# A conditioned transformer block on one core: gate rows over four column groups, and rules of their own for 13 of 64 attention steps

## The chip, the cores and the metric

The kernel runs on one core of a Trainium2 chip. The metric is the device time of one execution in microseconds (us). TensorE is written PE (PEld is its weight load), VectorE is DVE, ScalarE is ACT, GpSimd is POOL and SyncE is SP; SP issues the DMAs.

## What is computed

A transformer block whose two layer norms and two residual additions are modulated by a condition vector, one for each batch row. x is 8 x 1024 x 512, the condition 8 x 512, all in fp32; there are 16 heads of 32.

```python
mod = silu(condition) @ Wada + bada                # 8 x 3072
sh_a, sc_a, gt_a, sh_m, sc_m, gt_m = split(mod, 6, axis=1)
xm = layernorm(x) * (1 + sc_a[:, None]) + sh_a[:, None]
x  = x + gt_a[:, None] * attention(xm)             # causal, 16 heads; its output is @ Wproj + bproj
xm = layernorm(x) * (1 + sc_m[:, None]) + sh_m[:, None]
x  = x + gt_m[:, None] * (gelu(xm @ W1 + b1) @ W2 + b2)
```

The change touches how gt_a and gt_m, the two rows called gates, are made, and in which order the instructions of some attention steps are issued. What is computed stays the same.

## The kernel before, in words

**Tiling.** The tokens are worked through in 16 blocks of 512: block n is half n % 2 of batch row n // 2. Each block has four attention steps (n, g), g = 0 to 3, of four heads each, 64 steps in all. Beside attention there is linear work: the products for q, k and v, for the projection and for the two layers of the MLP. They are made as Strassen products from sums of weight quarters and sums of activations, by the helper `matmul` (L233), which puts four products on the four column groups of PE's array, 32 output rows each.

**An attention step.** It makes scores to find the row maxima: `scores_at_once` (L1784) multiplies on PE (L1791), adds the causal mask on DVE (L1805) and reduces on DVE (L1808). `split_maxima` (L1813) splits the maxima into three bf16 parts with four small operations (L1827 to L1830) on POOL or DVE, whichever the model says is done sooner. `maxima_rows` (L1838) turns them to rows on PE (L1846). `weights_T` (L1861) makes the scores again, transposed, with the maxima subtracted by a product of their own (L1872, L1884), and ACT takes the exponential (L1897); POOL clears the part over the diagonal (L1902). `weigh` (L1914) multiplies by v (L1925). POOL adds up the weights (`add_weights`, L2010), and `finish` (L1935) makes the denominators on PE (L1946). A "unit" is one such tile of scores or weights.

**PSUM.** Scores and transposed scores share one tile of four banks, called st, so they take turns; the output of `weigh` has one bank (po); linear work, maxima rows, denominators and gates share three banks.

**What sets the order.** The order of instructions on every engine is fixed when the program is built. While it issues instructions, the kernel's Python keeps a model of the time at which each engine is free (`now`, `note` and its kin, `due`, L70 to L160). Three rules in it matter here.

- `either` (L179) puts an elementwise sum on DVE or POOL. It goes to DVE only if DVE would be done earlier by more than `margin`, 1000 ns (L186); in the last step the margin is -2000.
- `step_aside` (L1651) is called ahead of each group of attention's instructions on PE. While the modelled wait of that group (`own`) is longer than that of the linear work that is ready (`other`), it issues linear work first. When linear work is behind its due time, attention goes ahead only if `other > own + 100`, and otherwise if `own <= max(other, 50)`.
- The list `plan` (L281) says in which window of blocks each linear step and each gate is made, and `costs` (L370) what each is reckoned at.

**The gates.** `gates` (L565) runs twice, for kinds a and m, during the first steps of block 0. It multiplies the activated condition (8 rows, as weights of 128 x 8) by the raw weights, in eight products of 256 columns, all on one column group and with 8 rows of output (L582). The bias comes by DMA as an 8-row broadcast (L571), is added on DVE while the bank is read (L222), and for kind a a second row, gate times the projection's bias (L574), is made on DVE. The rows are kept in DRAM, and `gate_broadcasts` (L598) loads the row of one batch row to all 128 partitions, 256 KB at a time: two rows for a and one for m, for each of 8 batch rows. `settle` (L1337) multiplies the MLP's output by the gate and adds it to the residual, both through `either`.

Of the kernel before, what the change touches and what calls it, by code (L numbers as in the profile page):

```python
# [22 lines left out]
def kernel(  # L23
# [128 lines left out]
    def note_pe(ns, form, reads=(), writes=()):  # L152
        now["PE"] = max(now["PE"], due(reads, writes))
        if shape[0] != form:
            shape[0] = form
            now["PE"] += SWITCH
        note("PE", ns, reads)
        spent[0] += ns
        for k in writes:
            written[k] = now["PE"] + PIPE  # L160
# [15 lines left out]

    margin = [1000]

    def either(out, a, b, op, reads, writes):  # L179

        n = 1
        for d in out.shape[1:]:
            n *= d
        on_dve, on_pool = 60 + 1.24 * n, 120 + 2.28 * n
        t = due(reads, writes)
        if max(now["DVE"], t) + on_dve + margin[0] < max(now["POOL"], t) + on_pool:  # L186
            nc.vector.tensor_tensor(out, a, b, op)
            note("DVE", on_dve, reads, writes, port=True)
        else:
            nc.gpsimd.tensor_tensor(out, a, b, op)  # L190
            note("POOL", on_pool, reads, writes)
# [29 lines left out]
    def combine_out(out, bank, src, other, reads=(), writes=(), op=ALU.add, last=True):  # L221
        nc.vector.tensor_tensor(out, src, other, op)  # L222
        note("DVE", 690, [("l", bank), *reads], writes)
        live[bank] = not last
# [142 lines left out]
        return []  # L367

    order = [at for w in range(-1, NB + 1) for step in plan[w] for at in pieces_of(step)]
    costs = {"at": 16 * TR, "mt": 16 * TR, "gates": 4 * MM, "mod": 4 * MM}  # L370
    costs["at"] = 0
    costs.update({kind: 14 * MM for kind in ("k", "q", "v", "u", "proj")})

# [181 lines left out]
    def half(i, size):  # L555
        return slice(i * size, (i + 1) * size)
# [8 lines left out]
    def gates(kind):  # L565

        i, bias = GATES[kind]
        at = take(4)
        part = {kf: halves(j) for kf, j in zip(RAW, at)}
        b_gate = tmp.tile([P, D], F32, tag="y", name=f"b_gate_{kind}")[:B, :]  # L570
        nc.sync.dma_start(b_gate, bada[i * D : (i + 1) * D].unsqueeze(0).to_broadcast([B, D]))  # L571
        if bias is not None:
            b_out = tmp.tile([P, D], F32, tag="y", name=f"b_out_{kind}")[:B, :]
            nc.sync.dma_start(b_out, bias.unsqueeze(0).to_broadcast([B, D]))  # L574
        yield [], [BANK]
        bank = lin_bank()
        ps = banks[bank][:B, :]
        for fh in range(2):
            for k in range(NC):
                if fh + k:  # L580
                    yield [], []
                nc.tensor.matmul(  # L582
                    ps[:, half(fh, HB)], condT[:, k, :B], part[k // 2, fh][:, k % 2, :],
                    start=fh + k == 0, stop=k == NC - 1, skip_group_check=True,
                )
                note_pe(2 * COLUMN * HB, "columns", [], [("l", bank)])
        release(*at)
        combine_out(b_gate, bank, ps, b_gate)
        made = [(f"g{kind}", b_gate)]
        if bias is not None:  # L590
            nc.vector.tensor_tensor(b_out, b_out, b_gate, ALU.mult)
            note("DVE", 700, port=True)
            made.append((f"gb{kind}", b_out))
        for name, row in made:
            kept_rows[name] = kept.tile([B, D], F32, tag=f"kept_{name}", name=f"kept_{name}")
            nc.sync.dma_start(kept_rows[name], row)

    def gate_broadcasts(b, kind):  # L598

        for name in [name for name in (f"g{kind}", f"gb{kind}") if name in kept_rows]:  # L600
            row = rowp.tile([P, D], F32, tag=f"row{name}", name=f"row_{name}_{b}")
            nc.sync.dma_start(row, kept_rows[name][b : b + 1, :].to_broadcast([P, D]))
            gate_rows[name] = row


# [577 lines left out]
        return y_keys[kind]  # L1183
    LANDING = 6000

    def add_to(xt, other, reads, writes, op=ALU.add):
        either(xt, xt, other, op, [*reads, *writes], writes)

    def half_sums(n, t):

# [146 lines left out]
    def settle(n, f, t, y, ky):  # L1337

        c = half(f, HB)
        gate = gate_rows["gm"][:, c].unsqueeze(1).to_broadcast([P, 2, HB])  # L1340
        keys = [("xr", n, 2 * t), ("xr", n, 2 * t + 1)]
        add_to(y, gate, [("row", "gm")], [ky], ALU.mult)
        add_to(residual[n][:, half(t, 2), c], y, [ky], keys)

    def store(n, t):
        b, h = blocks[n]
# [300 lines left out]
    def until(condition):  # L1647
        while not condition():
            work()

    def step_aside(reads, writes):  # L1651


        while threads():
            if linear_wait() == NEVER:
                hurry()
            own, other = wait_of((reads, writes)), linear_wait()
            if done_linear[0] < stream["due"]:
                if other > own + 100:
                    break  # L1660
            elif own <= max(other, 50):
                break
            work()
        while BANK in writes and bank_at() == NEVER:
            work()
        run_jobs()
        run_pool_jobs()
        run_transfers()
        run_preparation()
# [2 lines left out]


    TRIANGLE = [[0], [1, 3], [2]]
    groups = [(n, g) for n in range(NB) for g in range(NC)]

    def score_units(n, g):
# [335 lines left out]
    def attend():  # L2013
        previous = None
        for n in range(NB):
# [21 lines left out]
            written["free for k", n + 1] = 0.0  # L2037
            written["free for xr", n - 1] = 0.0
            for g, k, n_slots, upto in slots:
                if (n, g) == groups[-1]:  # L2040
                    margin[0] = -2000
                parts = weight_units(n, g)[k]
                while rows_due and any((n, part[3]) not in m_rows for part in parts):
                    maxima_rows()
                pT, slot = weights_T(n, g, parts)
                run_excursions(1)
                pace(exp_need(parts))
                maxima_rows()
                if previous is not None:
                    close(*previous)  # L2050
                for i in (n, n + 1) if h == 0 else (n,):
                    written["free for v", i] = 0.0
                if k > 0:
                    add_weights(n, g, [part for part in parts if part[3] == g], pT, slot)
                previous = (n, g, parts, pT, slot, k == n_slots - 1)
                if (n, g, k) == (0, NC - 1, n_slots - 1):

                    next_scores()
                    close(*previous)
                    previous = None  # L2060
                while unit_at[0] < upto:
                    ns = score_need(*units[unit_at[0]])
                    next_scores()
                    if h == 0:
                        run_excursions(1)
                    pace(ns)
                if previous is None:
                    maxima_rows()
# [125 lines left out]
```

## Time and profile before

| | us |
| --- | --- |
| median of 3 runs | 3460.41 |
| lowest and highest | 3459.74, 3460.67 |
| the profiled execution's own time | 3463.39 |
| span of its profile | 3461.7 |
| granted TensorE clock | 1.00 |

The span goes from the first to the last instruction that the profiler recorded; the execution's own time lies 1.7 us around it. A row of a timeline gives start, length, engine, line of the kernel, operation, output<-inputs, shapes and count; in square brackets stands how long the engine sat idle before it and what released it. Matmuls overlap, so their starts are the better measure of how fast they follow each other. An fp32 product counts as two instructions on PE. "Idle time" of a group is that of its engine just before it.

### The profile page before, as it was taken

Reading aid. Unit: us, or ns where it says so; the run is one execution under the profiler, and the core shown is the slowest. Engines: PE = TensorE matmul, PEld = TensorE weight load, DVE = VectorE, ACT = ScalarE, POOL = GpSimd, SP = SyncE. Lnnn points to the kernel's source line nnn. Section 1 sums busy time; section 2 is a strip of 40 time slices with the busy share of each in tenths; the row PEclk is TensorE's granted clock in tenths of the full one; section 3 lists DMA queues with packets and bytes.
Section 4 is the critical chain, followed back from the end, with each engine's and each line's share of the span. In section 5 each row is a group of like instructions: output and inputs, shape, how many; then the busy total and the mean of one; then the engine's idle time right before and its main releaser. Section 6 shows DMA issues by size and latency. Waiting matters only on the chain.

```text
span 3461.7 us, 122760 instructions
## 1 busy us (share of the span) xinstructions
PE 3420.8 (99%) x55538; PEld 1775.8 (51%) x55538; DVE 2068.1 (60%) x2304; ACT 1289.5 (37%) x1424; POOL 1939.0 (56%) x2092
## 2 busy tenths in 40 slices
PE   8999999999999999999999999999999999999999
PEld 5544554455544554455554455454554545545555
DVE  6765666646566465664657546575466755556454
ACT  2345244343243433434333352433524334242431
POOL 3666757756267472774626755277553775446520
PEclk9999999999999999999999999999999999999999
DMA  7832434345544455444544445444464444633344
GB/s 230 277 124 87 122 113 130 103 126 150 172 136 129 128 151 159 135 139 130 162 145 136 136 133 169 138 134 136 132 177 134 130 146 122 192 110 102 117 144 136
DMA packets 380429, 490.71 MB, mean 142 GB/s; under 512 B 28436, under 2 KB 236364, under 8 KB 379908
## 3 DMA queue, kind: packets, MB, share of 16 engines
q1 hardware_dynamic: 379712, 482.59, 46.4%
q8 instruction: 437, 7.16, 0.8%
q14 instruction: 84, 0.69, 0.1%
q10 hardware_dynamic: 196, 0.28, 0.0%
HBM read 429.22 MB, written 53.53 MB: 139 GB/s over the span
## 4 chain that ended last, share of the span: by engine, by line
PE 89%; DVE 4%; DMA 3%; ACT 2%; issue 1%; POOL 1%; SPq 0%; DVEq 0%; ACTq 0%; POOLq 0%
PE bank L233 61%; PE sc L1791 8%; PE po L1925 7%; PE st L1884 7%; PE st L1872 3%; DVE mx L1808 2%; PE bank L1946 2%; DMA w<-kept_up_S 1%; ACT pT L1897 1%; DMA xm_m<-turned_m 1%; DVE sc L1805 1%; PE bank L1846 1%; DVE hT L1378 0%; ACT hT L1309 0%; PE bank L887 0%
## 5 line engine op out<-in xcount | busy, mean ns | idle before, releaser
L2010 POOL TENSOR_TENSOR pT<-pT,pT 128x256 f32<-128x256 f32 (+3 forms) x1254 | 1218.8, 1007 | 159.6 <-ACT pT L1897 121.9
L1897 ACT ACTIVATE pT<-st 128x2048 f32<-128x2048 f32 x288 | 541.1, 1879 | 1007.8 <-PE st L1884 892.6
L233 PE MATMUL bank<-w,hT 128*32 128x256 f32 x14336 | 814.4, 380 | 0.0
L1808 DVE TENSOR_REDUCE mx<-sc 128x4 f32<-128x2048 f32 (+3 forms) x384 | 665.5, 1754 | 196.3 <-PE sc L1791 190.2
L233 PEld LDWEIGHTS bank<-w,hT 128*32 128x32 f32 x14336 | 453.8, 110 | 357.8 <-issue 74.2
L233 PE MATMUL bank<-xm_m,w 128*32 128x256 f32 x8192 | 499.2, 380 | 1.5 <-issue 1.0
L233 PE MATMUL bank<-t_m,w 128*32 128x256 f32 x6144 | 383.8, 380 | 0.8 <-DMA w<-kept_up_S 0.4
L1902 POOL TENSOR_SCALAR_AFFINE_SELECT pT<-pT 128x512 f32<-128x512 f32 x256 | 181.0, 725 | 359.0 <-ACT pT L1897 357.3
L233 PEld LDWEIGHTS bank<-xm_m,w 128*32 128x32 f32 x8192 | 255.5, 110 | 229.9 <-issue 64.3
L1791 PE MATMUL sc<-kT,qT 32*128 32x512 f32 (+3 forms) x3072 | 329.1, 520 | 3.2 <-DVE mx L1808 3.0
L1805 DVE TENSOR_TENSOR sc<-sc,mask 128x1024 f32<-128x1024 f32 (+1 forms) x160 | 162.7, 1017 | 250.5 <-PE sc L1791 174.0
L1925 PE MATMUL po<-pT,v 128*32 128x512 f32 (+3 forms) x3072 | 304.8, 491 | 0.0
L1884 PE MATMUL st<-qT,kT 32*128 32x512 f32 (+3 forms) x3072 | 300.0, 486 | 0.0
L233 PEld LDWEIGHTS bank<-t_m,w 128*32 128x32 f32 x6144 | 189.9, 110 | 177.3 <-issue 53.1
L233 PE MATMUL bank<-xm_a,w 128*32 128x256 f32 x3968 | 239.5, 380 | 1.8 <-ACT xm_a L902 1.1
L190 POOL TENSOR_TENSOR qT<-top,rec 128x512 f32<-128x512 f32 x59 | 77.3, 1310 | 280.5 <-ACT rec L1964 277.5
L222 DVE TENSOR_TENSOR hT<-bank,u_u 128x512 f32<-128x512 f32 x192 | 130.1, 686 | 150.4 <-PE bank L233 147.4
L1791 PEld LDWEIGHTS sc<-kT,qT 32*128 32x128 f32 x3072 | 129.4, 183 | 159.7 <-issue 58.0
L233 PE MATMUL bank<-w,qT 128*32 128x256 f32 (+1 forms) x3008 | 188.9, 389 | 2.3 <-DVE p_proj L214 2.3
L233 PE MATMUL bank<-t_a,w 128*32 128x256 f32 x2944 | 179.4, 380 | 0.0
L233 PEld LDWEIGHTS bank<-xm_a,w 128*32 128x32 f32 x3968 | 126.7, 110 | 98.0 <-issue 16.1
L1309 ACT ACTIVATE hT<-hT,cols 128x512 f32<-128x512 f32 x256 | 164.1, 711 | 23.1 <-DVE hT L222 22.4
(246 smaller groups left out, 3414.8 us busy)
## 6 DMA issues: line engine op xcount, KB each, us to landing
w<-in_L_cond_W_dram SPq DMA_DIRECT2D x384, 256.0 KB
w<-kept_up_S SPq DMA_DIRECT2D x256, 256.0 KB
w<-kept_down_S SPq DMA_DIRECT2D x256, 256.0 KB
w<-kept_qkv_S SPq DMA_DIRECT2D x180, 256.0 KB
w<-in_L_cond_Wqkv_dram SPq DMA_DIRECT2D x147, 256.0 KB
hat<-in_x_dram SPq DMA_DIRECT2D x64, 256.0 KB
xr<-in_x_dram SPq DMA_DIRECT2D x64, 256.0 KB
out_dram<-xr SPq DMA_DIRECT2D x64, 256.0 KB
```

The lines of the kernel that those rows point to most:

```text
L222: nc.vector.tensor_tensor(out, src, other, op)
L233: nc.tensor.matmul(ps[r], columns, rhs, start=start, stop=stop, skip_group_check=True)
L1309: nc.scalar.activation(hT[:, i, :], hT[:, i, :], AF.Gelu, bias=cols[:, O_B1 + f : O_B1 + f + 1])
L1791: nc.tensor.matmul(sc[:, j, c0 : c0 + w], qTs[n][r, gg, ts(qt, P)], keys_of(n, kh)[r, gg, :w], start=True, stop=True, skip_group_check=True,)
L1805: nc.vector.tensor_tensor(place, place, shape_of.to_broadcast(place.shape), ALU.add)
L1808: nc.vector.tensor_reduce(maxima[n, gg][:, kh, qt, :], sc[:, :, c0 : c0 + w], axis=AX.X, op=ALU.max)
L1872: nc.tensor.matmul(st[:, j, c0 : c0 + w], minus_ones[r, :], row[r, TB - w :], start=(c0 == 0), stop=False, skip_group_check=True,)
L1884: nc.tensor.matmul(st[:, j, c0 : c0 + w], kT[r, gg, ts(k % NTT, P)], qT[r, gg, TB - w :], start=False, stop=True, skip_group_check=True,)
L1897: nc.scalar.activation(pT[:, :, :used], st[:, :, :used], AF.Exp, scale=scale)
L1902: nc.gpsimd.affine_select(diagonal, diagonal, pattern=[[0, HPG], [1, P]], compare_op=ALU.is_ge, fill=0.0, base=0, channel_multiplier=-1,)
L1925: nc.tensor.matmul(po[r, TB - w :], v[:, k % NTT, g * P + j * hd : g * P + (j + 1) * hd], pT[:, j, c0 : c0 + w], start=(k == 0), stop=last ...
L2010: nc.gpsimd.tensor_tensor(into, into, pT[:, j, c0 : c0 + w], ALU.add)
```

## The change

It has four parts.

1. **Gates over four column groups.** `gates` makes, for each quarter of the columns, a product of 128 columns with 32 rows of output on its own column group (16 products for each kind, the condition now spread over all its 32 columns). The bias is no longer added on DVE: it comes by DMA as one row of 1 x 512 and is added by products with a row of ones (`spread_rows`, four products for each row; for kind a also four that spread the projection's bias beside it). DVE copies the 128 x 128 result, and for kind a multiplies the second by the first. The tile kept in DRAM is 128 x 128, and the broadcast of one batch row reads four pieces of 128 numbers. The planner reckons a gate at 2 MM in place of 4.
2. **Own rules for 13 steps.** `MANNER` gives 13 of the 64 steps a margin and a `leaning`. A leaning of 300 lets attention go ahead of linear work when its modelled wait is up to 300 ns longer than before the change. All other steps keep (1000, 0).
3. **Slack.** `either` can be given a `slack` that stands in for the margin.
4. `settle` uses a slack of 0 in block 0.

Below this text lines of after.py are some 17 to 22 higher than those of before.py from the attention on.

```diff
--- before.py
+++ after.py
@@ -176,14 +176,14 @@
 
     margin = [1000]
 
-    def either(out, a, b, op, reads, writes):
+    def either(out, a, b, op, reads, writes, slack=None):
 
         n = 1
         for d in out.shape[1:]:
             n *= d
         on_dve, on_pool = 60 + 1.24 * n, 120 + 2.28 * n
         t = due(reads, writes)
-        if max(now["DVE"], t) + on_dve + margin[0] < max(now["POOL"], t) + on_pool:
+        if max(now["DVE"], t) + on_dve + (margin[0] if slack is None else slack) < max(now["POOL"], t) + on_pool:
             nc.vector.tensor_tensor(out, a, b, op)
             note("DVE", on_dve, reads, writes, port=True)
         else:
@@ -367,7 +367,7 @@
         return []
 
     order = [at for w in range(-1, NB + 1) for step in plan[w] for at in pieces_of(step)]
-    costs = {"at": 16 * TR, "mt": 16 * TR, "gates": 4 * MM, "mod": 4 * MM}
+    costs = {"at": 16 * TR, "mt": 16 * TR, "gates": 2 * MM, "mod": 4 * MM}
     costs["at"] = 0
     costs.update({kind: 14 * MM for kind in ("k", "q", "v", "u", "proj")})
 
@@ -567,39 +567,56 @@
         i, bias = GATES[kind]
         at = take(4)
         part = {kf: halves(j) for kf, j in zip(RAW, at)}
-        b_gate = tmp.tile([P, D], F32, tag="y", name=f"b_gate_{kind}")[:B, :]
-        nc.sync.dma_start(b_gate, bada[i * D : (i + 1) * D].unsqueeze(0).to_broadcast([B, D]))
-        if bias is not None:
-            b_out = tmp.tile([P, D], F32, tag="y", name=f"b_out_{kind}")[:B, :]
-            nc.sync.dma_start(b_out, bias.unsqueeze(0).to_broadcast([B, D]))
+        added = [("g", bada[i * D : (i + 1) * D])] + ([] if bias is None else [("gb", bias)])
+        rows = []
+        for name, v in added:
+            row = tmp.tile([P, TB], F32, tag="y", name=f"b_{name}{kind}")[:1, :]
+            nc.sync.dma_start(row, v.unsqueeze(0))
+            rows.append(row)
         yield [], [BANK]
         bank = lin_bank()
-        ps = banks[bank][:B, :]
-        for fh in range(2):
-            for k in range(NC):
-                if fh + k:
-                    yield [], []
+
+        def spread_rows(r, start, stop):
+            for j in range(HPG):
                 nc.tensor.matmul(
-                    ps[:, half(fh, HB)], condT[:, k, :B], part[k // 2, fh][:, k % 2, :],
-                    start=fh + k == 0, stop=k == NC - 1, skip_group_check=True,
+                    banks[bank][j * hd : (j + 1) * hd, ts(r, P)], ones[:1, :hd], rows[r][:, ts(j, P)],
+                    start=start, stop=stop, skip_group_check=True,
                 )
-                note_pe(2 * COLUMN * HB, "columns", [], [("l", bank)])
+            note_pe(2 * COLUMN * P, "columns", [], [("l", bank)])
+
+        for k in range(NC):
+            for j in range(HPG):
+                nc.tensor.matmul(
+                    banks[bank][j * hd : (j + 1) * hd, :P], condT[:, k, :],
+                    part[k // 2, j // 2][:, k % 2, ts(j % 2, P)],
+                    start=k == 0, stop=False, skip_group_check=True,
+                )
+            note_pe(2 * COLUMN * P, "columns", [], [("l", bank)])
+            yield [], []
         release(*at)
-        combine_out(b_gate, bank, ps, b_gate)
-        made = [(f"g{kind}", b_gate)]
+        for r in range(len(rows)):
+            spread_rows(r, r > 0, True)
+        made = tmp.tile([P, TB], F32, tag="y", name=f"gates_{kind}")
+        gate = made[:, :P]
+        nc.vector.tensor_copy(gate, banks[bank][:, :P])
+        note("DVE", 250, [("l", bank)], [("gates", kind)])
         if bias is not None:
-            nc.vector.tensor_tensor(b_out, b_out, b_gate, ALU.mult)
-            note("DVE", 700, port=True)
-            made.append((f"gb{kind}", b_out))
-        for name, row in made:
-            kept_rows[name] = kept.tile([B, D], F32, tag=f"kept_{name}", name=f"kept_{name}")
-            nc.sync.dma_start(kept_rows[name], row)
+            nc.vector.tensor_tensor(made[:, P : 2 * P], banks[bank][:, P : 2 * P], gate, ALU.mult)
+            note("DVE", 250, [("l", bank)], [("gates", kind)])
+        live[bank] = False
+        for r, (name, _) in enumerate(added):
+            there = kept.tile([P, P], F32, tag=f"kept_{name}{kind}", name=f"kept_{name}{kind}")
+            kept_rows[name + kind] = there
+            nc.sync.dma_start(there, made[:, ts(r, P)])
 
     def gate_broadcasts(b, kind):
 
         for name in [name for name in (f"g{kind}", f"gb{kind}") if name in kept_rows]:
             row = rowp.tile([P, D], F32, tag=f"row{name}", name=f"row_{name}_{b}")
-            nc.sync.dma_start(row, kept_rows[name][b : b + 1, :].to_broadcast([P, D]))
+            of_b = kept_rows[name].rearrange("(j r) c -> r j c", r=hd)[b]
+            nc.sync.dma_start(
+                row.rearrange("p (j c) -> p j c", c=P), of_b.unsqueeze(0).to_broadcast([P, NC, P])
+            )
             gate_rows[name] = row
 
 
@@ -1183,8 +1200,8 @@
         return y_keys[kind]
     LANDING = 6000
 
-    def add_to(xt, other, reads, writes, op=ALU.add):
-        either(xt, xt, other, op, [*reads, *writes], writes)
+    def add_to(xt, other, reads, writes, op=ALU.add, slack=None):
+        either(xt, xt, other, op, [*reads, *writes], writes, slack)
 
     def half_sums(n, t):
 
@@ -1339,8 +1356,9 @@
         c = half(f, HB)
         gate = gate_rows["gm"][:, c].unsqueeze(1).to_broadcast([P, 2, HB])
         keys = [("xr", n, 2 * t), ("xr", n, 2 * t + 1)]
-        add_to(y, gate, [("row", "gm")], [ky], ALU.mult)
-        add_to(residual[n][:, half(t, 2), c], y, [ky], keys)
+        slack = 0 if n == 0 else None
+        add_to(y, gate, [("row", "gm")], [ky], ALU.mult, slack)
+        add_to(residual[n][:, half(t, 2), c], y, [ky], keys, slack=slack)
 
     def store(n, t):
         b, h = blocks[n]
@@ -1648,6 +1666,8 @@
         while not condition():
             work()
 
+    leaning = [0]
+
     def step_aside(reads, writes):
 
 
@@ -1656,9 +1676,9 @@
                 hurry()
             own, other = wait_of((reads, writes)), linear_wait()
             if done_linear[0] < stream["due"]:
-                if other > own + 100:
+                if other > own + 100 - leaning[0]:
                     break
-            elif own <= max(other, 50):
+            elif own <= max(other, 50) + leaning[0]:
                 break
             work()
         while BANK in writes and bank_at() == NEVER:
@@ -1672,6 +1692,7 @@
 
 
     TRIANGLE = [[0], [1, 3], [2]]
+    MANNER = {(0, 1): (1000, 300), (0, 3): (1000, 300), (1, 3): (-1000, 0), (2, 0): (-1000, 0), (2, 1): (2500, 0), (3, 1): (0, 0), (4, 0): (1000, 300), (6, 0): (1000, 300), (8, 0): (1000, 300), (10, 0): (1000, 300), (12, 1): (2500, 0), (14, 3): (0, 0), (3, 3): (2500, 300)}
     groups = [(n, g) for n in range(NB) for g in range(NC)]
 
     def score_units(n, g):
@@ -2037,6 +2058,7 @@
             written["free for k", n + 1] = 0.0
             written["free for xr", n - 1] = 0.0
             for g, k, n_slots, upto in slots:
+                margin[0], leaning[0] = MANNER.get((n, g), (1000, 0))
                 if (n, g) == groups[-1]:
                     margin[0] = -2000
                 parts = weight_units(n, g)[k]
```

## The prediction

> **What bounds the kernel now.** I read the head of the page first, then the chain that ended last.
>
> ```profile
> span 3461.7 us, 122760 instructions
> ...
> PE 3420.8 (99%) x55538; PEld 1775.8 (51%) x55538; DVE 2068.1 (60%) x2304; ACT 1289.5 (37%) x1424; POOL 1939.0 (56%) x2092
> ...
> PEclk9999999999999999999999999999999999999999
> ...
> PE 89%; DVE 4%; DMA 3%; ACT 2%; issue 1%; POOL 1%; SPq 0%; DVEq 0%; ACTq 0%; POOLq 0%
> ```
>
> TensorE (PE) is busy for 3420.8 of 3461.7 us, at full granted clock throughout, and the chain is PE for 89%. No other engine is above 60%. Only two things can shorten this program: less work on PE, or less of the 40.9 us in which PE stands idle. The busy times in three stretches (each row: length, then busy time and instructions of PE, PEld, DVE, ACT and POOL, clock, DMA share, GB/s) say where those 40.9 us lie.
>
> ```profile
> 0.00:89.20 89.20, 74.94 (x1196) 45.56 (x1197) 55.86 (x88) 24.89 (x35) 34.81 (x53) 1.00 0.69 227
> 89.20:3457.70 3368.50, 3345.82 (x54343) 1730.19 (x54342) 2011.42 (x2216) 1264.58 (x1389) 1904.20 (x2040) 1.00 0.47 139
> 3457.70:3461.70 4.00, 0.00 (x0) 0.00 (x0) 0.84 (x2) 0.00 (x0) 0.00 (x0) 1.00 0.52 195
> ```
>
> Start-up holds 14.3, the last store 4.0, and the 3368.5 us between them 22.7: over 64 attention steps about a third of a microsecond each. So the prize of any reordering is 22.7 us at most. The same view over the 13 steps that get rules of their own (the first of them, and the sum) says how much lies inside them.
>
> ```profile
> 89.20:115.80 26.60, 24.75 (x389) 13.54 (x389) 20.19 (x23) 9.69 (x12) 13.17 (x20) 1.00 0.78 261
> ...
> sum 537.20, PE 532.65 PEld 278.97 DVE 334.93 ACT 216.81 POOL 297.01; mean PE 40.97 PEld 21.46 DVE 25.76 ACT 16.68 POOL 22.85
> ```
>
> They lose 537.20 - 532.65 = 4.55 us in all. A rule also shifts what the next steps find, so what it is worth must be looked for behind its step as well. PE's waits, grouped (total us, times, longest), name the kinds:
>
> ```profile
> PE st L1872 <- DVE mx L1808: 8.1, 13, 1.9
> PE bank L1846 <- POOL mcols L1830: 5.9, 7, 1.6
> PE bank L233 <- DVE p_proj L214: 2.3, 5, 0.5
> ```
>
> The first is the shared score tile: PE may not write the next one before VectorE (DVE) has reduced the last. The second is the maxima rows, which wait for the split on GpSimd (POOL); the third is the projection, which waits for a copy out of PSUM.
>
> **The gate products, a term on PE alone.** The listing of line 582 and the timeline of PE (start, length to the modelled end, count) give both prices.
>
> ```profile
> L582 PE MATMUL bank<-w,condT x32: 378/379/383, 87.4 to 157.9; 128*8 128x256 f32 x32
> ```
> ```profile
> 90.84 1.67 PE L582 MATMUL bank<-w,condT 128*8 128x256 f32 x7
> 92.35 0.38 PE L582 MATMUL bank<-w,condT 128*8 128x256 f32 x1
> ...
> 104.79 0.72 PE L523 MATMUL bank<-w,condT 128*32 128x128 f32 x10
> 105.44 0.40 PE L1872 MATMUL st<-mrow,minus_ones 32*128 32x384 bf16 x8
> ...
> 1685.66 1.69 PE L233 MATMUL bank<-w,hT 128*32 128x256 f32 x28
> 1687.17 1.04 PE L1946 MATMUL bank<-pT,ones 128*32 128x512 f32 x8
> ...
> 2970.31 0.41 PE L1846 MATMUL bank<-ident_b,mcols 128*32 128x128 bf16 x16 [0.52 <-POOL mcols L1830]
> ```
>
> Removed: 32 instructions (each fp32 product is two) on one column group, a new one every 1.51/7 = 0.216 us: 6.9 us. Added: 16 + 16 products of 128 columns and 8 + 4 that spread the bias rows, 44 products or 88 instructions over four column groups. Such a mixture at 256 columns starts one every 1.51/28 = 0.054 us, so at 128 columns 0.027 (the maxima rows do 128 columns in 0.41/16 = 0.026): 2.4 us. The dearest row for 128 columns is line 523's, 0.65/10 = 0.065, a change of form included: 5.7 us. So the term lies between -1.2 and -4.5; I take **-4.5**, since the maxima rows are the nearest in width and in column groups.
>
> The Trainium skill (page "TensorE: Matmul & The Clock Gate", section "Back-to-back issue gap") gives about 81 ns for each 128-column matmul in a stream of weight load and matmul pairs. By it the 88 would take 7.1 us, an estimate from that page, and the gates would save nothing. The rows above disagree, with 0.026 and 0.027 where four column groups take turns.
>
> The two DVE operations per gate become 128x128 and cheaper. The broadcast reads four pieces of 512 B per partition in place of one of 2 KB: 24 loads of 128 x 3 more packets, 9216 on 380429. With the queue at 46.4% (row below) I cost that at nothing; its cover is the idle half of the queue. What is new is that PE reads the bias rows, which come by DMA:
>
> ```profile
> q1 hardware_dynamic: 379712, 482.59, 46.4%
> ```
> ```profile
> 80.25 2.05 SPq L990 DMA_DIRECT2D prep_up<-in_L_cond_W_dram  x4
> 82.39 0.41 SPq L393 DMA_DIRECT2D w<-kept_qkv_S  x1
> 82.84 0.33 SPq L571 DMA_DIRECT2D b_gate_a<-in_L_cond_bada_dram  x1
> 83.22 0.29 SPq L574 DMA_DIRECT2D b_out_a<-in_L_cond_bproj_dram  x1
> ```
>
> Five loads of 256 KB stand ahead of them: 1.3 MB at the 227 GB/s of that stretch is 5.8 us, so they land near 89; by the built order PE first needs them between 88 and 89, after the sixteen products. Behind a waiting product would stand all of PE. I bound this at 0 to 3 us for each gate and take 0: in the next stretch, quoted above, the queue moved 261 GB/s, by which they land near 88.2.
>
> **The moved steps.** In both programs I counted in the built order the PE work between the instruction that a waiter depends on and the waiter, with the spacings of the trace (0.054 us for a linear instruction, 1.14 for a score unit, 0.11 for a change of form, an estimate from 104.79: 0.65 less ten times 0.054). Where more lies between, the wait shrinks by as much. PE's order is the same in over twenty of the steps, and their waits are taken to stay. The waits with more work ahead of them:
>
> ```profile
> 115.81 0.40 PE L1872 MATMUL st<-mrow,minus_ones 32*128 32x512 bf16 x4 [1.87 <-DVE mx L1808]
> ...
> 444.59 0.64 PE L233 MATMUL bank<-xm_a,w 128*32 128x256 f32 x8 [0.70 <-ACT p_k L217]
> ...
> 794.76 0.64 PE L233 MATMUL bank<-w,qT 128*32 128x256 f32 x8 [0.48 <-DVE p_proj L214]
> ...
> 1327.31 1.14 PE L1791 MATMUL sc<-kT,qT 32*128 32x512 f32 x8 [2.02 <-DVE mx L1808]
> ...
> 1672.81 0.40 PE L1872 MATMUL st<-mrow,minus_ones 32*128 32x384 bf16 x8 [0.55 <-DVE mx L1808]
> ...
> 2495.61 0.64 PE L233 MATMUL bank<-w,qT 128*32 128x256 f32 x8 [0.48 <-DVE p_proj L214]
> 2522.05 0.40 PE L1872 MATMUL st<-mrow,minus_ones 32*128 32x384 bf16 x8 [0.56 <-DVE mx L1808]
> ...
> 2891.09 0.40 PE L1872 MATMUL st<-mrow,minus_ones 32*128 32x384 bf16 x8 [0.66 <-DVE mx L1808]
> ```
>
> - 115.81, step (0,2): 16 linear instructions and a change of form more, 0.97 of the 1.87 go.
> - 444.59, step (2,1): 32 linear instructions more, all 0.70 go.
> - 794.76 to 2495.61, four projections at the start of blocks 4, 8, 10 and 12: a score unit now comes between, 4 x 0.48 = 1.9 go.
> - 1327.31, step (6,2): 16 linear instructions more, 0.86 of 2.02 go.
> - 1672.81 to 2522.05, second step of blocks 8, 10 and 12: 56 to 72 more, 3 x 0.56 = 1.7 go.
> - 2891.09, step (14,0): 24 more, 0.66 go. 2970.31 (quoted above): 64 more, 0.52 go.
>
> Together **-7.3**. The other direction:
>
> ```profile
> 143.75 0.40 PE L1872 MATMUL st<-mrow,minus_ones 32*128 32x512 bf16 x4 [0.51 <-DVE mx L1808]
> ...
> 1622.25 0.41 PE L1846 MATMUL bank<-ident_b,mcols 128*32 128x128 bf16 x16
> ...
> 1696.08 0.41 PE L1846 MATMUL bank<-ident_b,mcols 128*32 128x128 bf16 x16 [0.52 <-POOL mcols L1830]
> ```
> ```profile
> 1616.10 0.27 POOL L1830 TENSOR_TENSOR mcols<-rest,mcols 128x16 bf16<-128x16 f32 x1
> ...
> 1694.96 1.07 POOL L1830 TENSOR_TENSOR mcols<-rest,mcols 128x16 bf16<-128x16 f32 x1
> ```
>
> Step (0,3) loses 16 linear instructions and gains a change of form ahead of its wait: +0.76. The maxima rows of (8,3) and of (10,3), which wait already (1696.08), lose 16: +0.86 each. The maxima rows of the second steps of blocks 4, 6, 8 and 10 move up from some 11.3 us behind the last score to 4.8 to 5.25. At 1622.25 they come 5.9 us after the split's end at 1616.37; some 6.05 earlier they wait 0.2, four times: 0.8. Together **+3.3**. Beneath nothing this term can't go, since less work stands ahead; above, each split can be stretched, as at 1694.96 (1.07 against 0.27 us): two such instructions add 1.6, six sites 9.6.
>
> The margins and the slack of block 0 move single sums between DVE and POOL: over the whole program DVE has 7 instructions more and POOL 4 fewer. Both are below 61% busy, so I cost the sums themselves at nothing; the cover is PE's queue, and where it ends is the list above.
>
> The Trainium skill (page "SBUF — State Buffer", section "🔬 SBUF: two separate sides") says that a DVE operation with two SBUF inputs and a POOL operation exclude each other on a shared port pair. The stretched split agrees; what that makes of a margin that favours DVE is in the rival on the splits, priced from the rows.
>
> **Sum.** -4.5 - 7.3 + 3.3 = -8.5. Against the profiled execution's own 3463.4 that is 3454.9. That execution lies 3.0 over the median of the runs, 3460.4; from the median it is **3451.9**. What a measurement of this kernel can tell from no change is about 0.2%, 6.9 us: faster is below 3453.5, slower above 3467.3.
>
> **Rivals.**
>
> *More goes than I counted* (0.17). The order shows distances, not what DVE and POOL do meanwhile. If the +3.3 don't come and a wait that stays in my count goes too, such as this one of 1.60,
>
> ```profile
> 843.45 0.41 PE L1846 MATMUL bank<-ident_b,mcols 128*32 128x128 bf16 x16 [1.60 <-POOL mcols L1830]
> ```
>
> the sum is -4.5 - 7.3 - 1.6 = -13.4: 3447.0. For it: the rules sit where waits sit. Against it: 843.45 has 5.25 us ahead of it in both programs.
>
> *Only the gates' saving stays* (0.17). Every wait that goes comes back a unit later, since one score tile serves scores and weights in turn and DVE still has the same reductions to make: -4.5, 3455.9. For it: 8.1 us of waits in 13 pieces all end on the same reduction.
>
> *The gates save nothing* (0.05). With 0.081 us per instruction in place of 0.027 the term is +0.2 and the sum -3.8: 3456.6. The rows of four column groups speak against it. This is the issue gap of the Trainium skill's page "TensorE: Matmul & The Clock Gate" applied to the whole gate.
>
> *The splits queue behind POOL's additions* (0.13), which makes it slower. Six maxima rows (four moved up, two with less ahead) wait for a split on POOL, which takes its work in order; a batch of four additions ahead of it costs 4 x 1.007 = 4.0 us:
>
> ```profile
> L2010 POOL TENSOR_TENSOR pT<-pT,pT 128x256 f32<-128x256 f32 (+3 forms) x1254 | 1218.8, 1007 | 159.6 <-ACT pT L1897 121.9
> ```
>
> Six times 4.0 is 24.2; less 4.5 and 7.3 it is +12.4: 3472.8. It decides from the third site on (11.8 us are to be used up), and is past the bound of 6.9 with the fifth. For it: the 1.60 at 843.45 with just 5.25 us ahead. Against it: at 1616.10 the split came undelayed.
>
> **How the numbers follow.** Forecast 0.48, with a range of its own from 3448 to 3457 (up by the gates' dearest row, 3.3, and 2 for the bias rows; down by the 3.3 that may not come). By the bound it gives 0.34 faster and 0.14 the same; the first rival 0.17 faster; the second 0.03 faster and 0.14 the same; the third 0.05 the same; the last 0.09 slower and 0.04 the same. So 0.54 faster, 0.37 the same, 0.09 slower. The range 3443 to 3461 leaves out the far ends of the first rival (half the idle time that is left) and nearly all of the last.
>
> **What would show it.** Right: line 582's successors take under 3 us in all; PE busy falls by about 4; the waits at the sites listed shrink, the group of st behind mx by 4 us, that of p_proj to the one of block 15. Wrong: PE waiting for the DMA of a bias row; the group of maxima rows behind POOL over 10 us; or PE's idle time between 89 and the end not falling below 20 us.

## The result, and the profile after

The changed kernel takes 3485.17 us (median of 6 runs, 3480.89 to 3492.47) against 3460.07 for the kernel before (3457.86 to 3461.48): a ratio of 1.0075, 95% interval 1.0062 to 1.0088. The forecast was 3451.9, the range ended at 3461, and slower than the bound had a chance of 0.09. The sign was wrong.

The head of the page after:

```profile
span 3486.8 us, 122848 instructions
...
PE 3428.3 (98%) x55594; PEld 1776.9 (51%) x55594; DVE 2072.1 (59%) x2311; ACT 1284.8 (37%) x1419; POOL 1916.6 (55%) x2088
...
q1 hardware_dynamic: 389270, 482.69, 46.2%
q8 instruction: 438, 7.18, 0.8%
```

PE does not fall by 4 us, it rises by 7.5 although the gates have become cheaper, and its idle time rises from 40.9 to 58.5. The groups of PE's waits in the changed kernel (total us, times, longest) say what is new:

```profile
PE bank L233 <- issue: 13.4, 5, 5.5
PE bank L1867 <- POOL mcols L1851: 9.9, 8, 1.6
PE sc L1812 <- issue: 5.1, 1, 5.1
PE bank L233 <- DVE p_proj L214: 4.7, 1, 4.7
...
PE st L1893 <- DVE mx L1829: 4.1, 10, 1.4
```

The last row is as forecast: the waits behind the score reductions fall from 8.1 by 4 us. The first and the third were in no case of the prediction: 18.5 us in which PE waited "for issue", that is, for nothing that the profile shows as a releaser (1.0 us in the kernel before). A sign of being wrong that the prediction had set does show: between 89.20 and 3483.00 us PE stands idle for 41.9 us, where it had asked for less than 20. One such place in the timeline of PE, with the timeline of SP's issues ahead of it:

```profile
2179.03 0.49 SPq L617 DMA_DIRECT2D row_ga<-kept_ga  x1
2179.77 0.55 SPq L617 DMA_DIRECT2D row_gba<-kept_gba  x1
2183.33 1.29 SPq L391 DMA_DIRECT2D w<-in_L_cond_W_dram  x2
2184.99 18.60 SPq L393 DMA_DIRECT2D w<-kept_up_S  x4
```
```profile
2192.99 1.13 PE L1812 MATMUL sc<-kT,qT 32*128 32x512 f32 x6
2199.27 2.07 PE L1812 MATMUL sc<-kT,qT 32*128 32x512 f32 x2 [5.15 <-issue]
2201.27 1.93 PE L233 MATMUL bank<-xm_m,w 128*32 128x256 f32 x16
```

PE stops in the middle of a unit of scores, after six of its eight instructions. Fifteen microseconds earlier SP issued the two gate broadcasts of a batch row, and the four ordinary loads behind them took 18.60 us to issue. (At the same place of the kernel with whole rows, the first experiment below, they took 10.53; the 18.60 hold PE's own stop.) The windows of the same stretch (length, busy time of PE, PEld, DVE, ACT, POOL, clock, DMA share, GB/s), and the DMA queues between 2181 and 2196 us:

```profile
2176.00:2181.00 5.00, 5.00 (x100) 3.03 (x96) 2.05 (x3) 0.00 (x0) 0.64 (x1) 1.00 0.75 240
2181.00:2194.00 13.00, 13.00 (x182) 5.53 (x174) 6.49 (x6) 4.32 (x6) 0.64 (x1) 1.00 0.34 68
```
```profile
q1 hardware_dynamic: 1349, 1.03, 33.6%
q14 instruction: 1, 0.01, 0.2%
```

The DMA engines fall from 240 to 68 GB/s for 13 us while being busy for a third of the time only: they wait. (With whole rows the 13 us at this place moved 143 GB/s.) And queue q8 is missing from the second answer. Its packets of 16 KB bring PE's instructions, as their size tells: 438 of them, one in 8 us on average, are 7.18 MB, which is 64.5 bytes for each of the 111188 matmuls and weight loads, and no other queue of instructions moved more than 0.69 MB. The trace has one at 2176.85 and the next at 2197.05. PE ran dry at 2194, 16 us after the last block had come in. The other stops of over a microsecond named issue are alike: at all five PE starts again 1.3 to 1.7 us after a block has landed, and stopped 14.6 to 17.3 us after the landing of the block before that one. That the broadcasts hold up these blocks is inferred from the two times standing together; the experiments below test it by changing the broadcasts alone.

Behind such a stop the clock is halved. The windows of the four stretches in which the trace has a granted clock of 0.5 ahead of the kernel's end:

```profile
167.68:174.50 6.82, 4.37 (x44) 2.50 (x47) 0.80 (x2) 0.00 (x0) 1.68 (x2) 0.50 1.02 362
1338.45:1345.27 6.82, 4.77 (x31) 1.54 (x35) 1.61 (x1) 0.00 (x0) 0.16 (x1) 0.50 0.30 110
2198.61:2205.43 6.82, 6.16 (x42) 2.47 (x46) 2.89 (x2) 0.00 (x0) 0.00 (x0) 0.50 0.37 124
3147.52:3154.34 6.82, 5.79 (x44) 2.10 (x48) 3.95 (x4) 0.00 (x0) 0.00 (x0) 0.50 0.00 0
```

PE is busy for 21.1 us in them and gets half of that done, a loss of 10.5. They go with the idle times of 5.47, 4.41, 5.15 and 4.65 us; behind idle times of 2.16 and 1.19 the clock stays at 1.00. The Trainium skill (page "TensorE: Matmul & The Clock Gate", section "🔬 Part 1: The HAM clock gate (the "warmup" mystery)") has the clock halved after an idle window of about 3.4 us. The trace agrees on the window's length: each stretch lasts twice 3.41 us, and their starts lie 343, 252 and 278 times 3.413 us apart. It does not agree on a window that is idle throughout: the stretch at 1338.45 begins 2.35 us after PE stopped, so PE was still busy for 1.06 us of the 3.41 us ahead of it. Nor is there one idle time from which the clock falls: in the run with pieces 32 KB apart (below) an idle time of 2.02 us was followed by 3.41 us at half clock, and one of 2.02 us in the kernel before by none.

### The profile page after: what moved, and what is told of

Read it like the earlier page. It is cut to its first block, busy times and chain, and to the rows that moved or that the text cites. A ratio compares the mean times of both kernels' runs of the same rounds, so it can differ in the third digit from the quotient of the medians.

```text
span 3486.8 us, 122848 instructions
## 1 busy us (share of the span) xinstructions
PE 3428.3 (98%) x55594; PEld 1776.9 (51%) x55594; DVE 2072.1 (59%) x2311; ACT 1284.8 (37%) x1419; POOL 1916.6 (55%) x2088
## 3 DMA queue, kind: packets, MB, share of 16 engines
q8 instruction: 438, 7.18, 0.8%
## 4 chain that ended last, share of the span: by engine, by line
PE 90%; DVE 3%; ACT 3%; DMA 1%; issue 1%; POOL 1%; SPq 0%; DVEq 0%; ACTq 0%; POOLq 0%
PE bank L233 63%; PE sc L1812 9%; PE po L1946 7%; PE st L1905 7%; PE st L1893 3%; DVE mx L1829 2%; PE bank L1967 2%; ACT pT L1918 1%; DMA xm_m<-turned_m 1%; DVE sc L1826 1%; ACT hT L1326 1%; PE bank L1867 0%; DMA w<-kept_up_S 0%; PE bank L904 0%; ACT L170 0%
```

## Experiments

Where an order is called unchanged or the same, the instructions on PE, DVE, ACT and POOL stand in the same order; that holds for every kernel below in which only the place of the rows in DRAM differs from one of the two kernels. "Pair" is the two broadcasts of kind a, 1024 packets of 512 B, and its duration goes from the first to the last of these packets in the trace, at the second batch row.

**First four: which part of the change.** The forecast's own mechanism stands against two others: the pieces of 512 B (A), or the moved loads (B).

Whole rows in DRAM, all else as changed:

```diff
-            there = kept.tile([P, P], F32, ...)
+            there = kept.tile([hd, D], F32, ...)
-            nc.sync.dma_start(there, made[:, ts(r, P)])
+            nc.sync.dma_start(there.rearrange("r (j c) -> j r c", c=P), made[:, ts(r, P)])
...
+            nc.sync.dma_start(row, kept_rows[name][b : b + 1, :].to_broadcast([P, D]))
```

> The changed kernel with one thing undone: the gate rows are kept in DRAM as whole rows of 512 numbers, so that the broadcast reads 2 KB at a time again; every instruction of PE, DVE, ACT and POOL is that of the changed kernel. Theory A (the pieces): the 24 broadcasts in pieces of 512 B hold up the DMA queues, PE's instruction blocks come late, PE stands for about 5 us and then runs at half clock for 6.8 us; without the pieces no wait of PE called issue is over 2 us and the time is 3450 to 3456, or up to 3460 if the wait of 4.65 us of a projection in block 15 has another cause. Theory B (the order): the rules of 13 steps move loads and additions so that they collide with PE's instruction blocks, whatever the size of the pieces: 3480 to 3490 as before the repair.

Measured: 3451.08 us, ratio 0.9977 (0.9968 to 0.9986). The stalls named issue are gone, the clock is 1.00. This is within 1 us of the time that was forecast for the change. PE's waits and the page's head:

```profile
span 3448.6 us, 122848 instructions
...
PE 3414.2 (99%) x55594; PEld 1772.0 (51%) x55594; DVE 2067.5 (60%) x2311; ACT 1285.9 (37%) x1419; POOL 1919.8 (56%) x2088
```
```profile
PE bank L1864 <- POOL mcols L1848: 9.9, 8, 1.6
...
PE st L1890 <- DVE mx L1826: 4.1, 10, 1.4
...
PE sc L1809 <- DVE mx L1826: 2.0, 3, 0.9
```

With the same order, then, the layout of three small tensors in DRAM is worth 38.2 us of span between the two profiles (3486.8 less 3448.6) and 34.1 between the medians. Of the 38.2, 24.1 are PE idle time, with 18.5 in the stops named issue and 4.7 in the wait for p_proj (whose cause stays open, see the end of the next part), and 14.1 are PE busy time, with 10.5 in the halved clock.

The gates alone (`MANNER = {}`, `slack = None`; pieces as changed):

> The changed kernel with no step having rules of its own and no slack: only the gates over four column groups, with broadcasts in pieces of 512 B. Theory A: the stalls stay, 3 or so of 8 to 9 us each, less 4.5 for the gate products: 3472 to 3485. Theory B: 3455 to 3457.

Measured: 3493.65, ratio 1.0094 (1.0080 to 1.0108). The stalls are there without any moved step; B falls. The time is 8.7 us over the upper end that A gave; 5.1 of them are a wait for a score reduction, which stands in the run with whole rows and neither rules nor slack (below) as well.

The rules alone (the function `gates` and its broadcast as before):

> The changed kernel with the gates of the kernel before: only the rules of 13 steps and the slack, with broadcasts of 2 KB. Theory A: no late instruction blocks, 3453 to 3460. Theory B: 3480 to 3490.

Measured: 3462.51, ratio 1.0007 (0.9998 to 1.0016): no stalls, but no gain either, 2.5 us over the upper end that A gave.

The kernel before with pieces of 512 B:

```diff
-            kept_rows[name] = kept.tile([B, D], F32, ...)
+            kept_rows[name] = kept.tile([NC, B, P], F32, ...)
```

> The kernel before with one thing added: the gate rows lie in DRAM as four pieces of 128 numbers for each batch row, apart from each other, so that each broadcast moves 512 pieces of 512 B; instructions on the engines are those of the kernel before. Theory A: 3475 to 3495, with PE waits called issue of about 5 us some 12 to 15 us behind the pair of broadcasts at the start of a batch row, and half clock behind each. Theory B: 3460, no change.

Measured: 3461.63, ratio 1.0002 (0.9993 to 1.0011). The page has 389717 packets, 9288 more than before, and nothing happens. So theory A falls as it was put: the size of the pieces and their number alone cost nothing. What was different is that the pieces of a batch row lay 4 KB apart (8 rows of 512 B) and in the changed kernel 16 KB (32 rows).

**Theory C: the distance in DRAM.** The same edit of the kernel before, with 32 rows:

```diff
+            kept_rows[name] = kept.tile([NC, hd, P], F32, ...)
```

> The kernel before with each broadcast in 512 pieces of 512 B as in the run with pieces alone, but the four pieces of a batch row 16 KB apart in DRAM, as in the changed kernel, in place of 4 KB. Theory C (the place in DRAM): pieces 16 KB apart are read slowly, the pair of broadcasts takes 13 to 15 us in place of 8, PE's instruction blocks come late: 3475 to 3495. Theory B2 (pieces and the changed order together, the distance without meaning): 3458 to 3463.

Measured: 3485.24, ratio 1.0068 (1.0053 to 1.0083), the whole loss of the change with none of its gates, rules or moved instructions. PE's waits of this run:

```profile
PE bank L233 <- issue: 10.1, 3, 6.2
...
PE bank L1949 <- issue: 6.0, 1, 6.0
```

The changed kernel with 8 and with 33 rows for each column group (both also store the rows in use with four DMAs in place of one):

> The changed kernel with pieces of 512 B as it has them, but only the 8 rows in use are kept, so that the four pieces lie 4 KB apart. Theory C: the pair takes 8 us, no waits called issue over 2 us, 3449 to 3455. Theory B2: 3478 to 3492.

> The changed kernel with 33 rows for each column group in DRAM, so that the pieces lie 16.5 KB apart in place of 16. If it is the round distance, the pair takes about 8 us and the time is 3449 to 3456; if it is pieces far from each other, or pieces as such, 3478 to 3492 as before.

Measured: 3454.51, ratio 0.9983 (0.9974 to 0.9991), and 3450.82, ratio 0.9973 (0.9963 to 0.9983). Theory B2 falls, C stands, and it is the round number that hurts, not the distance: half a kilobyte more and the loss is gone. These two and the run with whole rows are faster than both kernels, and than the one before by 0.2 to 0.3%.

More distances, on the kernel before:

> The kernel before with broadcasts in 512 pieces of 512 B, the four pieces of a batch row 8 KB apart. If the place in DRAM repeats every 16 KB, the four pieces lie on two places: between the runs with 4 KB (3461.6) and 16 KB (3485.2), 3462 to 3475, the pair of broadcasts in 9 to 12 us. If any distance over 4 KB is slow: 3477 to 3495.

> As the run with 8 KB, but 24 KB apart. If the place repeats every 16 KB, the same two places as with 8 KB: 3462 to 3475. If the distance as such makes it slow: 3477 to 3495 or more.

> As the run with 8 KB, but 32 KB apart. If the place repeats every 16 KB, all four pieces on one place as with 16 KB: 3477 to 3495. If 16 KB alone is bad: 3459 to 3463.

> The kernel before with broadcasts in 512 pieces of 512 B, 12 KB apart. If multiples of 8 KB are what is slow (8, 16 and 24 KB gave 3485 to 3487): the pair in 8 us or less, 3458 to 3464. If any distance from 8 KB to 24 KB other than 16.5 is: 3480 to 3490.

> As the run with 12 KB, but 4.5 KB apart: if an odd number of 512 B between the pieces spreads them (as 16.5 KB did, 3.3 us for the pair against 7.8 at 4 KB), the pair takes 3 to 5 us, 3458 to 3463; if a small distance such as 4 KB is what is slow there, about 8 us, and the same time.

| distance | pair, us | time, us | ratio to before, 95% interval |
| --- | --- | --- | --- |
| 4.5 KB | 3.4 | 3460.36 | 1.0000 (0.9990 to 1.0009) |
| 4 KB | 7.9 | 3461.63 | 1.0002 (0.9993 to 1.0011) |
| 12 KB | 7.7 | 3461.95 | 1.0005 (0.9996 to 1.0015) |
| 32 KB | 11.5 | 3467.64 | 1.0019 (1.0009 to 1.0028) |
| 8 KB | 15.2 | 3487.39 | 1.0078 (1.0060 to 1.0097) |
| 24 KB | 15.3 | 3484.87 | 1.0070 (1.0054 to 1.0087) |
| 16 KB | 16.0 | 3485.24 | 1.0068 (1.0053 to 1.0083) |

A map that repeats every 16 KB is refuted: 8 and 24 KB should have been better than 16, and 32 KB as bad. What the rows show is that multiples of 8 KB are slow (32 KB less so), 4 and 12 KB cost no time, and the two distances that are an odd number of pieces, 9 and 33, are fastest. Why, no run shows. The 15 us from the second issue on, in the runs with 12 KB and with 8 KB:

```profile
461.22:476.22 15.00, 14.64 (x219) 7.71 (x212) 10.16 (x10) 6.32 (x8) 11.48 (x15) 1.00 0.45 114
```
```profile
463.64:478.64 15.00, 13.34 (x189) 6.68 (x180) 10.15 (x10) 6.32 (x8) 11.45 (x15) 1.00 0.35 66
```

Same loads, 114 against 66 GB/s, and with 8 KB PE has lost 1.3 us more by the end of the window. The table has one batch row; from the second to the eighth the pairs took 7.7 to 11.0 us at 4 and 12 KB, which costs nothing, 11.5 to 13.8 at 32 KB, which costs some, and 14.2 to 17.9 at 8, 16 and 24 KB, which costs the whole loss. That fits the 14.6 to 17.3 us after a block's landing at which PE ran dry. The Trainium skill (page "Runtime: NRT & Kernel Launch", section "🔬 Instruction fetch mechanics") says that an engine's instructions come by a DMA queue of its own in blocks of 16 KiB and that this is mostly hidden; the trace agrees on the blocks, and shows where the hiding ends.

**Is it the pair?** The changed kernel, 16 KB, with the two broadcasts one linear step apart from the second batch row on, which came to 18 to 23 us (order unchanged):

```diff
-        plan[w] = steps + rows_m + rows_a + ups[:i]
+        plan[w] = steps + rows_m + rows_a1 + ups[:1] + rows_a2 + ups[1:i]
```

> The changed kernel, pieces 16 KB apart as it has them, but from the second batch row on the two broadcasts of a pair are issued one linear step (some 30 us) apart; the order on PE, DVE, ACT and POOL is unchanged. If the late instruction blocks come from the length of time for which the pair holds the queue (13 to 15 us, where one broadcast takes 5 to 6): stalls remain only behind the first pair, 3452 to 3462. If each slow broadcast delays a block: 3475 to 3492 as before.

Measured: 3469.04, ratio 1.0028 (1.0017 to 1.0040), 16 us less than the changed kernel and 18 more than with 16.5 KB. The waits:

```profile
PE bank L233 <- issue: 11.7, 5, 5.9
```

The longest, 5.9, is behind the first pair, which was left together. The other four are of 1.1 to 2.1 us, and begin 12 to 19 us behind the issue of the second of the two broadcasts, and no halved clock follows them. So the answer lies between the two expectations: parting the pair removes most of the loss, but one slow broadcast, here of 7.6 to 8.3 us, can still make a block late by a microsecond or two. The time for which the queue is held is then not all of it, since pairs of up to 11.0 us at 4 KB made none late; what else counts stays open.

**The terms of the sum.** With whole rows, and neither rules nor slack:

> The kernel with whole rows of 2 KB and the gates over four column groups, no rules of its own for any step and no slack: the gates' products alone. By the forecast's term of 4.5: 3455 to 3457. If the rules were needed for the gain of the run with whole rows (3451): 3458 to 3462.

Measured: 3462.26, ratio 1.0007 (0.9998 to 1.0015). That is the second expectation within 0.3 us: the cheaper gates alone gain nothing, nor do the rules alone (3462.51), but both together gain 0.23%. The gates' work itself has become cheaper as forecast. The timeline of PE with whole rows, gate a:

```profile
85.70 1.06 PE L589 MATMUL bank<-w,condT 128*32 128x128 f32 x32
86.69 0.42 PE L581 MATMUL bank<-b_ga,ones 1*32 1x128 f32 x8
86.93 0.40 PE L581 MATMUL bank<-b_gba,ones 1*32 1x128 f32 x8
87.31 0.39 PE L1890 MATMUL st<-mrow,minus_ones 32*128 32x512 bf16 x4
```

48 instructions in 1.61 us, 0.034 each, with no wait for a bias row. But the planner now puts everything behind them at other times, and without the rules one place goes badly. PE, DVE and POOL in the run without rules:

```profile
391.63 0.61 PE L1890 MATMUL st<-mrow,minus_ones 32*128 32x512 bf16 x4 [5.09 <-DVE mx L1826]
```
```profile
385.46 1.51 DVE L187 TENSOR_TENSOR y_d<-y_d,row_gm 128x512 f32<-128x512 f32 x1
387.01 1.63 DVE L187 TENSOR_TENSOR xr<-xr,y_d 128x512 f32<-128x512 f32 x1
388.56 0.69 DVE L1823 TENSOR_TENSOR sc<-sc,mask 128x512 f32<-128x512 f32 x1
```
```profile
383.92 5.84 POOL L2028 TENSOR_TENSOR pT<-pT,pT 128x512 f32<-128x512 f32 x4
```

Two sums have gone to DVE ahead of the mask and the reduction that PE waits for, and beside POOL's additions they take 1.51 and 1.63 us. The wait of 5.09, with 6.83 us at half clock around its end, in which PE is busy for 4.07 and so loses another 2, eats more than the 4 us of the gates.

Four of the 13 rules taken out, with pieces 16.5 KB apart:

```diff
-    MANNER = {..., (4, 0): (1000, 300), (6, 0): (1000, 300), (8, 0): (1000, 300), (10, 0): (1000, 300), ...}
```

> The changed kernel with pieces 16.5 KB apart, and without the rules for the first steps of blocks 4, 6, 8 and 10. By the forecast's count these four rules remove 1.9 at the copies of the projections and about 1.7 at second steps, and add 0.9 to 1.6 at the maxima rows of the last steps of blocks 6, 8 and 10 (the profile with whole rows has 1.61 at each): nearly nothing in all, 3449 to 3453. If they carry the gain: 3455 to 3460.

Measured: 3451.99, ratio 0.9974 (0.9964 to 0.9983), against 3450.82 and 0.9973 with all 13. The prediction's terms for these four come to about -1 us, and the runs don't contradict them; a difference of that size is too small for these runs to show.

## Why the prediction was wrong

**The step that failed** is the one on the broadcasts: "9216 on 380429. With the queue at 46.4% (row below) I cost that at nothing; its cover is the idle half of the queue." The packets were counted rightly and cost nothing, as the run with pieces 4 KB apart shows. What was not looked at is where they lie. The change keeps 32 rows per column group where 8 are used, so the four pieces of a row are 16 KB apart, and 128 partitions read the same four places. At that distance the pair of the second batch row takes 13.5 us (16.0 in the kernel before with that layout) in place of 3.3 at 16.5 KB, the DMA engines' share falls while it is held up (0.75 to 0.34 ahead of 2194), and the idle half of a queue is no cover for that. The loss of this step, put at nothing, is 38.2 us between two profiles of the same order.

**What was left out of the cases** is that PE itself hangs on the queues: its instructions come in blocks by DMA, and behind the slow broadcasts the blocks came late. The prediction sought PE's new waits among semaphores alone. It also took an idle microsecond to cost a microsecond; each of the idle times of 4.4 us and more cost another two to three in halved clock.

**The rest of the sum came out, in part by luck.** Without the layout's fault the change takes 3451.1 and 3450.8 us against a forecast of 3451.9. From the profile before to the one with whole rows, however, PE's busy time falls by 6.6 us (forecast 4.5) and its idle time by 6.5 (forecast 4.0). Together that is 13.1; between the medians it is 9.7, since the profiled execution before lay 2.6 above its median of 3460.79 and that with whole rows 0.7 below its own. By the terms:

- Gates, -4.5: 0.034 us an instruction in place of 0.027, by which 88 take 3.0 and the term is -3.9. The bias rows' wait, taken at 0, is 0 at both gates. The 0.081 of the third rival does not occur.
- Waits that go: those at the copies of the projections are gone, the group of sc behind mx fell from 3.0 to 2.0 (forecast 0.86 less). The first two rows of PE's timeline with whole rows that wait for a reduction:

```profile
111.19 0.40 PE L1890 MATMUL st<-mrow,minus_ones 32*128 32x512 bf16 x4 [1.00 <-DVE mx L1826]
...
140.19 0.40 PE L1890 MATMUL st<-mrow,minus_ones 32*128 32x512 bf16 x4 [1.40 <-DVE mx L1826]
```

  Step (0,2) has 1.00 in place of 1.87 (forecast 0.97 less).
- Waits that come: step (0,3), the second row, has 1.40 in place of 0.51 (forecast 0.76 more). The 0.87 less and 0.89 more are near the 0.86 of the 16 linear instructions alone; the change of form, put at 0.11, was worked out with the spacing of 256 columns on a row of 128 columns, and doesn't show here. The maxima rows were under-sized: the group rose from 5.9 to 9.9 where the terms gave 2.0 more. The row of PE's timeline with whole rows for block 8's last step, with those of blocks 6 and 10 alike:

```profile
1261.83 0.41 PE L1864 MATMUL bank<-ident_b,mcols 128*32 128x128 bf16 x16 [1.61 <-POOL mcols L1848]
1685.54 0.41 PE L1864 MATMUL bank<-ident_b,mcols 128*32 128x128 bf16 x16 [1.61 <-POOL mcols L1848]
2109.99 0.41 PE L1864 MATMUL bank<-ident_b,mcols 128*32 128x128 bf16 x16 [1.61 <-POOL mcols L1848]
```

1.61 in place of 0.52 at blocks 8 and 10, 1.09 more each and not 0.86, and block 6 was not in the list. The waits of 0.2 at the four sites that moved up don't show.

**The rivals.** The one on the other side, splits queued behind POOL's additions, was right in its sign by luck and wrong in its mechanism: the group behind POOL is 9.9 us in the changed kernel and 9.9 with whole rows. "Only the gates' saving stays" had every wait come back; with whole rows the group of st behind mx stays at 4.1 us in place of 8.1, and the time is below the 3455.9 that it gave. The gates alone, without rules, gave nothing: the terms belong to one order and don't add up part by part.

**One thing stays open.** The wait of 4.65 us for p_proj in block 15, in the changed kernel's profile alone. DVE and POOL there, and DVE at the same place with whole rows:

```profile
3142.30 5.58 DVE L187 TENSOR_TENSOR qT<-t,qT 128x512 f32<-128x512 f32 x1 [4.16 <-PE bank L233]
3147.81 0.68 DVE L214 COPY p_proj<-bank 128x512 f32<-128x512 f32 x1
```
```profile
3137.90 5.54 POOL L2031 TENSOR_TENSOR pT<-pT,pT 128x384 f32<-128x384 f32 x8
...
3144.57 2.77 POOL L2031 TENSOR_TENSOR pT<-pT,pT 128x256 f32<-128x256 f32 x4
```
```profile
3111.57 0.87 DVE L187 TENSOR_TENSOR qT<-t,qT 128x512 f32<-128x512 f32 x1 [4.16 <-POOL pT L2028]
```

The same sum took 5.58 us beside POOL's additions and ended 0.5 us behind the last of them, where it took 0.87 in the other run. That POOL kept it out is what the rows suggest; it was not tried, nor why it came in between in the one run and not in the other.

## What to carry to other kernels

A tensor that is kept for re-reading has a price in where its pieces lie, not only in their size: work out the distance between the pieces of one load, and where all partitions read the same pieces keep it off multiples of 8 KB, or keep the row whole. A load that nobody waits for can still cost TensorE time, since the blocks of its instructions can come late behind it: when a wait is named "issue", look at the DMA rate in the 15 us ahead of it, and for the packets of the instruction queue. And sum terms only over an order that was built with all of them; the parts of a planned kernel don't add up one by one.

## What the runs showed of the hardware

- Broadcasts of 512 packets of 512 B that read four places 8, 16 or 24 KB apart run at a fraction of the rate of 4.5 or 16.5 KB: at the second batch row 15 to 16 us for a pair, on the kernel before, against 3.3 to 3.4. The Trainium skill (page "DMA: Bandwidth & Descriptors", section "🔬 Latency and other measured facts") reports the like for copies with row pitches of 512 KiB and more, restored by 4 KiB of padding; here 8 KB was enough to slow and 512 B to restore.
- PE lived for 14.6 to 17.3 us after a block's landing on the instructions that it had; a later block stopped it, once in the middle of a unit, and it went on 1.3 to 1.7 us after the landing.
- In the changed kernel's profile each idle time of 4.4 us or more went with 6.82 us at half clock, one of 2.16 didn't; in the run at 32 KB one of 2.02 us went with 3.41.
